# Rearranging the hand-over from an attention loop to a recurrence, and shortening the recurrence's warm-up

## Chip, cores and metric

One core of a Trainium2 chip runs the kernel. The metric is the device time of one execution in microseconds (us); the kernel before takes 3046.68 us, the median of 3 runs (3046.57 to 3047.66).

## The reference

The input x is 4 images of 128 channels by 64 x 64 positions (N = 4096 positions), float32. Cut to what matters, with the normalisations written as names:

```python
# layer 0: attention over positions, with gates, on group-normalised x
x = x + conv_bn(attention(q, k, v) * gate, Wp, sp, bp)
# layer 1: on tokens t = x with the channels last
t = t + softmax(q q^T) ln(t),  q = ln(t) @ W
# recurrence over the 4096 positions, for 4 images
Wx = batchnorm(ln(t) @ Wf.T) * gamma + beta      # statistics over all images and positions
y[i] = sigmoid(Wx[i] + V @ y[i-1]),  y[-1] = 0   # V is orthogonal (from a QR)
t = t + y                                        # the output, channels first again
```

The batch normalisation needs the mean and variance of all of Wx, so the recurrence can't start before the last attention block of the last image has gone through its layer norm and its product with Wf.

## The kernel before, in words

**Body.** For each image b the kernel does layer 0 (`layer0`, score products L238, weighted sums L476) and layer 1 (`layer1`, L726, L605, L618), 8 blocks of 512 positions each. Small jobs (normalising the next image, finishing a block) are kept in the lists `ahead` and `pending` and one is taken after each score block. Which of the emitted instructions an engine issues first is decided by a scheduler that goes by emission order and a time model, except inside a `manual_schedule` region, where every engine issues the region's instructions in the order in which they are emitted; where instructions from outside the region fall among them stays the scheduler's. `keep_in_program_order` pins one instruction behind what its engine has been given so far. Before, only the prologue (up to L797) is such a region.

**End chain.** When all parts of a block n of layer 1 are summed (`part`, L627), `finish(n)` emits four jobs: `tokens` (transposes L660, denominators L663 to L665, residual L667, layer norm L299, L300, POOL L145 and L146, L303), `turn` (transposes L680, copy by ScalarE L681, and `result`, which transposes on VectorE L275 and sends the block with 4 DMAs on SP's queue, L279) and `inputs` (product L689, statistics L690, copy L693 into `wxs`). Block 0 of the last image comes last; its jobs take their banks from the pool `ps_s`, those of the other blocks take the only bank of `ps_m`. So the jobs of blocks 2, 1 follow one another through that bank. Block 1's `turn` and `inputs` are still to run when block 0's `tokens` begins.

**Between chain and recurrence.** A first Sigmoid on ScalarE fetches the table (L827), three VectorE instructions compare all denominators with bounds (L829 to L831). Then the pools are closed and a new pool gives six PSUM banks; six products (L850) mark them as written so that later products can add to what VectorE puts there. VectorE joins the statistics (L854), POOL takes the inverse root (L145, L146), and VectorE makes `gain` and `bias` (L856 to L859).

**Recurrence.** The 4096 positions are cut into chunks of L = 32 positions that advance side by side: 4 images x 128 chunks. Each chunk first repeats the last W = 12 positions of the chunk before it as a warm-up, then does its own 32: 44 steps. A step is done in two halves of 2 images (256 columns): TensorE multiplies by V and adds into a bank that VectorE has preloaded with gain x input (`preload`, L873, two steps ahead, one instruction for each half), ScalarE applies the Sigmoid (L890). Step 0 has no product: `sigmoid(gain * wx + bias)` (L883), which is a start from y = 0. Three banks per half are used in turn. From warm-up's end plus 4 steps, VectorE adds finished results to the residual `t2s` (L900), one instruction of 512 columns for each step and four after the last one; `t2s` is loaded by 4 DMAs of 2 MB (L839) and leaves by 4 DMAs (L905), the first of which starts after the first of these last four sums. At the end (L909 to L913) the state that the warm-up reached is compared with the true one; where it differs by more than 2^-18, a `general` path recomputes everything.

**Start.** x arrives in 4 pieces of 1024 columns. While VectorE takes statistics of them, TensorE multiplies parts of x by the identity (`warm`, L781): four products ahead of the group mean's product L346, one behind it, two behind the variance's product L356. They read columns 0 to 511 of x. `normalise` (L362) overwrites these columns, then the first real product L369 reads them.

Of the kernel before, what the change touches and what calls it, by code (L numbers as in the profile page):

```python
# [10 lines left out]
F32 = mybir.dt.float32  # L11
I32 = mybir.dt.int32
AF = mybir.ActivationFunctionType
ALU = mybir.AluOpType
# [18 lines left out]
PAIRS = NT // 2  # L33
LAG = 2
SHIFT = 48.0
L, W = 32, 12
G = N // L
GB = QB // L

# [133 lines left out]
def fast(  # L173
# [10 lines left out]
    bias = keep.tile([P, 1], F32, name="bias")  # L184
    first_y = keep.tile([P, 1], F32, name="first_y")

    with ExitStack() as st:
        big = st.enter_context(tc.tile_pool(name="big", bufs=1))
        ep = st.enter_context(tc.tile_pool(name="ep", bufs=4))
        accp = st.enter_context(tc.tile_pool(name="accp", bufs=1))  # L190
        work = st.enter_context(tc.tile_pool(name="work", bufs=1))
        stat = st.enter_context(tc.tile_pool(name="stat", bufs=4))
        ps_s = st.enter_context(tc.tile_pool(name="ps_s", bufs=2, space=PSUM))
        ps_o = st.enter_context(tc.tile_pool(name="ps_o", bufs=3, space=PSUM))
        ps_m = st.enter_context(tc.tile_pool(name="ps_m", bufs=1, space=PSUM))

# [94 lines left out]
        def layernorm(src, dst):  # L293

            mv = stat.tile([P, NQ, 2], F32, tag="mv", name="mv")
            rstd = stat.tile([P, NQ], F32, tag="rstd", name="rstd")
            for j in range(NQ):
                s6 = stat.tile([P, 6], F32, tag="s6", name="s6")
                nc.vector.bn_stats(s6, src[j])  # L299
                nc.vector.bn_aggr(mv[:, j, :], s6)  # L300
            inv_sqrt(rstd, mv[:, :, 1], EPS_LN)
            for j in range(NQ):
                nc.vector.tensor_scalar(  # L303
                    dst[j], src[j], mv[:, j, 0:1], rstd[:, j : j + 1],
                    ALU.subtract, ALU.mult,
                )
# [244 lines left out]
        def layer1(b, h, qt):  # L551
# [84 lines left out]
            def finish(n):  # L636
                cs = bass.ts(n, QB)
                rinv = stat.tile([P, NQ], F32, tag="rinv", name="rinv")
                t = work.tile([P, 4, NQ, 32], F32, tag="t", name="t1", bufs=2)
                if b == B - 1 and n == 0:  # L640

                    one, two = (ep.tile([P, 2, QB], F32, tag="e", name="last") for _ in range(2))
                    h2, t1 = (one[:, r, :].rearrange("q (j c) -> q j c", j=NQ) for r in range(2))
                    th = two[:, 0, :]

                    def bank():
                        return ps_s.tile([P, 2, QB], F32, tag="s", name="ml")[:, 0, :]
                else:
                    h2 = work.tile([P, NQ, C], F32, tag="h2", name="h2")
                    th = work.tile([P, QB], F32, tag="th", name="th")  # L650
                    t1 = work.tile([P, NQ, C], F32, tag="og", name="t1b")

                    def bank():
                        return ps_m.tile([P, QB], F32, tag="m", name="m1")
                nc.sync.dma_start(t, t_d[b, n])

                def tokens():
                    m = bank().rearrange("q (j c) -> q j c", j=NQ)
                    for j in range(NQ):
                        nc.tensor.transpose(m[:, j, :], oacc[:, n, bass.ts(j, P)], ident)  # L660
                    at = (B + b) * NT + n * NQ
                    den = den_all[:, at : at + NQ]
                    nc.vector.tensor_reduce(den, m, AX.X, ALU.add)  # L663
                    nc.vector.tensor_scalar(den, den, 1.0 / C, None, ALU.mult)
                    nc.vector.reciprocal(rinv, den)  # L665
                    for j in range(NQ):
                        nc.vector.scalar_tensor_tensor(  # L667
                            t1[:, j, :].rearrange("q (p i) -> q p i", p=4),
                            m[:, j, :].rearrange("q (p i) -> q p i", p=4), rinv[:, j : j + 1],
                            t[:, :, j, :], ALU.mult, ALU.add,  # L670
                        )
                    layernorm(quarters(t1), quarters(h2))

                def result():
                    turn_out(t1.rearrange("q j (p i) -> q j p i", p=4), t2_d[b, :, cs])

                def turn():
                    m = bank()
                    for j in range(NQ):
                        nc.tensor.transpose(m[:, bass.ts(j, P)], h2[:, j, :], ident)  # L680
                    nc.scalar.copy(  # L681
                        th.rearrange("c (p j k) -> c j p k", j=NQ, p=4),
                        m.rearrange("c (j p k) -> c j p k", j=NQ, p=4),
                    )
                    result()

                def inputs():
                    m = bank()
                    nc.tensor.matmul(m, lhsT=wt["f"], rhs=th, start=True, stop=True)  # L689
                    nc.vector.bn_stats(bn_st[:, b * NB + n, :], m)  # L690
                    m = m.rearrange("p (g i s) -> p i g s", i=L // 2, s=2)
                    if b == B - 1:
                        nc.vector.tensor_copy(wxs[:, :, b, bass.ts(n, GB), :], m)  # L693
                    else:
                        wx = work.tile([P, L // 2, GB, 2], F32, tag="wx", name="wx")
                        nc.vector.tensor_copy(wx, m)
                        nc.sync.dma_start(wxs_d[b, :, :, bass.ts(n, GB), :], wx)

                if b == B - 1 and n == 0:
                    pending.appendleft(tokens)  # L700
                    pending.extend([turn, inputs])
                elif b == B - 1 and n < 4:
                    pending.extend([tokens, turn, inputs])
                else:
                    pending.extend([tokens, nothing, nothing, nothing, turn, inputs])
# [57 lines left out]
                        turned.append((clock + 4, n, a, t))  # L763
            while fifo:
                direct()
            pending.extend([reversed_products] * len(turned))

        def own_bank(_):
            return ps_m.tile([P, 512], F32, tag="m", name="mp")
# [8 lines left out]
        def warm(cols):  # L778

            m = ps_o.tile([P, QB], F32, tag="o", name="warm")  # L780
            nc.tensor.matmul(  # L781
                m[:, :cols], lhsT=ident, rhs=parts0[0][:, :cols], start=True, stop=True
            )

        for _ in range(4):
            warm(QB)
        for work_ in norm[:-2]:
            work_()
# [34 lines left out]
                ahead.popleft()()  # L823
        flush()


        tc.keep_in_program_order(nc.scalar.activation(first_y, shift, AF.Sigmoid))  # L827
        ok = big.tile([P, 2, 2 * B * NT], F32, tag="oacc", name="ok")
        nc.vector.tensor_scalar(ok[:, 0, :], den_all, DEN_LO, None, ALU.is_ge)  # L829
        nc.vector.tensor_scalar(ok[:, 1, :], den_all, DEN_HI, None, ALU.is_le)  # L830
        nc.vector.tensor_reduce(par_ok[:, 1:2], ok.rearrange("p a b -> p (a b)"), AX.X, ALU.min)  # L831


    with ExitStack() as st:
        scan = st.enter_context(tc.tile_pool(name="scan", bufs=1))
        ps_r = st.enter_context(tc.tile_pool(name="ps_r", bufs=1, space=PSUM))
        t2 = scan.tile([P, B, N], F32, name="t2s")
        for b in range(B):
            nc.sync.dma_start(t2[:, b, :], t2_d[b])  # L839
        y = scan.tile([P, L // 2, B, G, 2], F32, name="y")  # L840
        state = scan.tile([P, B, G + 1], F32, name="state")
        nc.gpsimd.memset(state[:, :, 0:1], 0.0)

        HB = B // 2
        banks = [[ps_r.tile([P, 512], F32, tag=f"r{s}{i}", name="ps_r") for i in range(3)] for s in range(2)]
        for s in range(2):
            for i in range(3):
                nc.tensor.matmul(  # L850
                    banks[s][i][:, : HB * G], lhsT=ident, rhs=wxs[:, 0, :HB, :, 0],
                    start=True, stop=True, skip_group_check=True,
                )
        nc.vector.bn_aggr(mv, bn_st.rearrange("p a b -> p (a b)"))  # L854
        inv_sqrt(gain, mv[:, 1:2], EPS_BN)
        nc.vector.tensor_mul(gain, gain, col(GAMMA))  # L856

        nc.vector.tensor_mul(bias, mv[:, 0:1], gain)
        nc.vector.tensor_sub(bias, col(BETA), bias)  # L859

        halves = [slice(s * HB, (s + 1) * HB) for s in range(2)]
        steps = list(range(L - W, L)) + list(range(L))

# [3 lines left out]
        def at(tile_, i, bs):  # L867
            return tile_[:, i // 2, bs, :, i % 2]

        def preload(k):  # L870
            if k < len(steps):
                for s, bs in enumerate(halves):
                    nc.vector.tensor_scalar(bank(k, s), at(wxs, steps[k], bs), gain, None, ALU.mult)  # L873

# [3 lines left out]
        for k, i in enumerate(steps):  # L878
            for s, bs in enumerate(halves):

                dst = state[:, bs, 1:] if k == W - 1 else at(y, i, bs)
                if k == 0:
                    nc.scalar.activation(dst, at(wxs, i, bs), AF.Sigmoid, bias=bias, scale=gain)  # L883
                    continue
                before = state[:, bs, :G] if k == W else at(y, i - 1, bs)
                nc.tensor.matmul(
# [7 lines left out]
            if k >= W:  # L894
                todo.extend((i - 3, b) for b in range(B) if i % 4 == 3)
                for j in range(len(todo) if i == L - 1 else min(1, len(todo))):
# [7 lines left out]
                    if i0 == L - 4:  # L904
                        nc.sync.dma_start(out[b], t2[:, b, :])  # L905


        gap = scan.tile([P, B, G - 1], F32, name="gap")
        nc.vector.tensor_sub(gap, state[:, :, 1:G], at(y, L - 1, slice(0, B))[:, :, : G - 1])  # L909
# [406 lines left out]
```

## Time and profile before

| | |
|---|---|
| median of 3 runs | 3046.68 us |
| profiled execution, its own time | 3047.56 us |
| its span, first to last instruction | 3045.7 us |
| TensorE busy | 2989.5 us, 98% of the span |
| VectorE, ScalarE, POOL busy | 1677.2, 1032.2, 221.0 us |
| last sum of layer 1's block 0 (L627) | 2941.69 us from the span's start |
| first Sigmoid of the recurrence (L883) | 2959.84 us |
| first step with a product: its Sigmoid (L890) | 2963.00 us |
| Sigmoid of the last step | 3018.27 us |
| first output DMA issued | 3019.60 us |
| end of the span | 3045.7 us |

A row of the timeline or of the chain of waits gives the start in us from the span's start, the duration, the engine, and what was written from what. PEld is TensorE's weight load. Each float32 product appears as two MATMUL records. PEclk is TensorE's granted clock as a share of full speed.

### The profile page before, as it was taken

The numbers are of one execution on the slowest core, as the hardware profiler recorded it, in microseconds if no ns is written. First come the engines' busy times: TensorE is split into PE (matmuls) and PEld (weight loads), VectorE is DVE, ScalarE is ACT, GpSimd is POOL, SyncE is SP. The second block draws the span as 40 slices with busy tenths as digits, with TensorE's granted clock in tenths as the row PEclk, the third lists the DMA queues.
The fourth block names the chain that finished last, engine by engine and source line by source line (L and its number), as shares of the span: only waits on it lengthen the run. The fifth ranks groups of instructions, "written<-read, shape, count | busy, mean of one in ns | idle before, by whom it ended". The sixth has DMA issues, their size and how long they took to land.

```text
span 3045.7 us, 31528 instructions
## 1 busy us (share of the span) xinstructions
PE 2989.5 (98%) x10720; PEld 1371.1 (45%) x10720; DVE 1677.2 (55%) x3114; ACT 1032.2 (34%) x1151; POOL 221.0 (7%) x215
## 2 busy tenths in 40 slices
PE   9999999999999999999999999999999999999985
PEld 4444444444444444444444444444444444444442
DVE  6666654434666664444466665443456666333356
ACT  3444432222344432222244443222234443222224
POOL 0011100000011110000011101000001111000000
PEclk9999999999999999999999999999999999999998
DMA  1112143434122123333311114343422113544333
GB/s 42 41 53 56 52 117 87 97 90 99 41 56 56 48 85 96 94 96 87 87 46 56 42 47 118 85 98 87 101 58 59 39 49 90 143 100 102 96 119 151
DMA packets 246986, 241.09 MB, mean 79 GB/s; under 512 B 90016, under 2 KB 162208, under 8 KB 245792
## 3 DMA queue, kind: packets, MB, share of 16 engines
q1 hardware_dynamic: 246816, 238.98, 29.6%
q8 instruction: 88, 1.44, 0.2%
q14 instruction: 82, 0.67, 0.1%
HBM read 65.80 MB, written 56.62 MB: 40 GB/s over the span
## 4 chain that ended last, share of the span: by engine, by line
PE 92%; DVE 3%; SPq 2%; ACT 1%; DMA 0%; issue 0%; POOL 0%; DVEq 0%; POOLq 0%; ACTq 0%
PE o L476 28%; PE o L605 15%; PE ps L238 14%; PE ps L726 14%; PE ot L618 12%; SPq L760 2%; PE m L267 1%; PE m L689 1%; PE mp L438 1%; PE ps L578 1%; PE mq L570 1%; PE mp L369 1%; PE mp L423 1%; DVE t2s L900 1%; DVE ps_r L873 1%; PE m L680 1%
## 5 line engine op out<-in xcount | busy, mean ns | idle before, releaser
L476 PE MATMUL o<-e,nxt 64*128 64x512 f32 x4096 | 973.1, 589 | 0.0
L240 ACT ACTIVATE e<-ps 128x1024 f32<-128x1024 f32 x512 | 520.9, 1023 | 687.1 <-PE ps L238 648.1
L247 DVE TENSOR_TENSOR acc<-acc,e 128x1024 f32<-128x1024 f32 x448 | 547.6, 1222 | 228.5 <-ACT e L240 212.4
L476 PEld LDWEIGHTS o<-e,nxt 64*128 64x128 f32 x4096 | 403.4, 187 | 482.9 <-issue 474.1
L238 PE MATMUL ps<-nxt 64*128 64x512 f32 x2048 | 541.6, 595 | 1.9 <-ACT e L592 0.8
L605 PE MATMUL o<-e,h 128*128 128x512 f32 x1160 | 537.0, 592 | 0.0
L730 ACT ACTIVATE e<-ps,shift 128x1024 f32<-128x1024 f32 x258 | 287.2, 1113 | 646.3 <-PE ps L726 357.9
L726 PE MATMUL ps<-qt 128*128 128x512 f32 x1032 | 482.9, 594 | 2.7 <-ACT qt L571 2.7
L618 PE MATMUL ot<-tt,h 128*128 128x512 f32 x888 | 400.9, 593 | 0.0
L733 DVE STREAM_TRANSPOSE dd<-e 128x512 f32<-128x512 f32 x444 | 281.7, 682 | 137.9 <-ACT e L730 83.7
L605 PEld LDWEIGHTS o<-e,h 128*128 128x128 f32 x1160 | 218.8, 190 | 268.2 <-issue 268.0
L238 PEld LDWEIGHTS ps<-nxt 64*128 64x128 f32 x2048 | 197.9, 187 | 231.0 <-issue 148.8
L726 PEld LDWEIGHTS ps<-qt 128*128 128x128 f32 x1032 | 189.9, 190 | 219.3 <-issue 190.8
L618 PEld LDWEIGHTS ot<-tt,h 128*128 128x128 f32 x888 | 167.8, 190 | 210.2 <-issue 205.3
L627 DVE TENSOR_TENSOR oacc<-oacc,ot 128x512 f32<-128x512 f32 x87 | 59.7, 687 | 288.4 <-PE ot L618 288.4
L145 POOL TENSOR_SCALAR rstd<-mv 128x4 f32<-128x4 f32 x64 | 14.5, 226 | 2374.9 <-DVE mv L300 2374.9
L532 DVE SCALAR_TENSOR_TENSOR t<-yt,rinv,t 128x128 f32<-128x128 f32 x128 | 36.5, 347 | 80.2 <-DMA yt<-turn_d 80.2
L493 POOL TENSOR_SCALAR xb<-xb,bpc 128x512 f32<-128x512 f32 x32 | 61.6, 1924 | 243.9 <-DMA xb<-in_x_dram 234.3
L543 POOL TENSOR_SCALAR h<-h 128x512 f32<-128x512 f32 x32 | 72.3, 2261 | 63.7 <-DVE d L275 61.7
L588 ACT ACTIVATE e<-ps,shift 128x512 f32<-128x512 f32 x32 | 22.0, 687 | 144.1 <-PE ps L584 133.8
L146 POOL TENSOR_TENSOR rstd<-rstd,mhalf 128x4 f32<-128x4 f32 x64 | 66.4, 1037 | 5.3
L629 DVE COPY oacc<-ot 128x512 f32<-128x512 f32 x24 | 16.6, 691 | 85.6 <-PE ot L618 85.5
(156 smaller groups left out, 1611.2 us busy)
## 6 DMA issues: line engine op xcount, KB each, us to landing
tt<-dd SPq DMA_DIRECT2D x1776, 64.0 KB, 2.0
turn_d<-d SPq DMA_DIRECT2D x384, 64.0 KB, 1.8
nxt<-in_x_dram SPq DMA_DIRECT2D x16, 512.0 KB, 5.6
xb<-in_x_dram SPq DMA_DIRECT2D x32, 256.0 KB, 3.3
t<-turn_d SPq DMA_DIRECT2D x32, 256.0 KB, 2.7
yt<-turn_d SPq DMA_DIRECT2D x32, 256.0 KB, 2.7
t_d<-t SPq DMA_DIRECT2D x32, 256.0 KB, 2.0
qt<-turn_d SPq DMA_DIRECT2D x32, 256.0 KB, 2.9
```

The costliest lines, as they stand in the source:

```text
L146: nc.gpsimd.tensor_tensor(dst, dst, mhalf[:, :n], ALU.pow)
L238: nc.tensor.matmul(ps[:, h, :], lhsT=lhsT, rhs=rhs, start=True, stop=True)
L240: nc.scalar.activation(e, ps, AF.Exp, scale=scale)
L247: nc.vector.tensor_tensor(acc, acc, e, ALU.add)
L476: nc.tensor.matmul(o[r], lhsT=v[rs, p + h * PAIRS, :], rhs=e[rs, h, :], start=(p == 0 and h == 0), stop=(p == PAIRS - 1 and h == 1),)
L493: biased = nc.gpsimd.tensor_scalar(xb, xb, bpc, None, ALU.add)
L543: nc.gpsimd.tensor_scalar(hn, hn, 1.0, None, ALU.add)
L605: nc.tensor.matmul(o, lhsT=h[:, NQ * a + 2 * i + half, :], rhs=e[:, half, :], start=(a == order(n)[0] and i == 0 and half == 0), stop=(a = ...
L618: nc.tensor.matmul(ot, lhsT=h[:, NQ * n + j, :], rhs=t[:, :, j, :, :].rearrange("q p k j -> q k p j"), start=(j == 0), stop=(j == NQ - 1),)
L726: nc.tensor.matmul(ps[:, half, :], lhsT=qt[:, bass.ts(at, P)], rhs=qt[:, bass.ts(n, QB)], start=True, stop=True,)
L730: nc.scalar.activation(e, ps, AF.Exp, bias=shift)
L733: nc.vector.transpose(d.rearrange("q f b k j -> q k b f j")[:, 2 * i + half], e[:, half, :].rearrange("q (b f j) -> q b f j", b=NQ, f=NQ),)
```

## The change

The kernel after differs in these places.

- **Warm-up:** W is 10 instead of 12, so 42 steps. Step 0 starts from y = 1/2: its bias is `first_bias`, which is `bias` plus V times a column of 1/2 (one product with one column, `of_half`).
- **Region:** after the last weighted sum of the last image a `manual_schedule` region begins; it is closed ahead of the recurrence. In it, in written order: block 0's `tokens`, `turn`, `inputs`, the product `of_half`, the table's Sigmoid, the joined statistics, the inverse root, the copy of block 0's inputs (now after the statistics: `last_inputs`), and five small VectorE operations that make `first_bias`, `gain` and `bias`.
- **Banks:** the loop's PSUM pools stay open. Block 0's jobs use `ps_o`. The recurrence's six banks are the two double banks of `ps_s`, one of `ps_o` and the one of `ps_m`; they are taken and marked in block 0's `tokens` right behind its transposes (`take_banks`), each mark being a product that reads the constant `bc`.
- **Products for the clock:** `busy(4)`, four products of 512 columns into one of these banks, after the marks and again after `of_half`. At the start `warm` reads columns 1536 to 2047 (the second piece), and two of its products stand ahead of the mean instead of four.
- **Joint scaled inputs:** where a step's two banks are the two of one `ps_s` tile (two steps of three) one VectorE instruction of 512 columns preloads both halves.
- **Layer norm:** `bn_aggr` of a tile is emitted one `bn_stats` later.
- **Block 1:** one empty job stands between its `tokens` and `turn`.
- **Denominator check:** emitted behind the recurrence.

```diff
-L, W = 32, 12
+L, W = 32, 10
...
+    half = keep.tile([P, 1], F32, name="half")
+    nc.gpsimd.memset(half, 0.5)
+    first_bias = keep.tile([P, 1], F32, name="first_bias")
...
-        ps_s = st.enter_context(tc.tile_pool(name="ps_s", bufs=2, space=PSUM))
-        ps_o = st.enter_context(tc.tile_pool(name="ps_o", bufs=3, space=PSUM))
-        ps_m = st.enter_context(tc.tile_pool(name="ps_m", bufs=1, space=PSUM))
+        ps_s = keep_ctx.enter_context(tc.tile_pool(name="ps_s", bufs=2, space=PSUM))
+        ps_o = keep_ctx.enter_context(tc.tile_pool(name="ps_o", bufs=3, space=PSUM))
+        ps_m = keep_ctx.enter_context(tc.tile_pool(name="ps_m", bufs=1, space=PSUM))
...
+            sums: deque = deque()
             for j in range(NQ):
                 s6 = stat.tile([P, 6], F32, tag="s6", name="s6")
                 nc.vector.bn_stats(s6, src[j])
-                nc.vector.bn_aggr(mv[:, j, :], s6)
+                sums.append((mv[:, j, :], s6))
+                if j > 0:
+                    nc.vector.bn_aggr(*sums.popleft())
+            nc.vector.bn_aggr(*sums.popleft())
...
                     def bank():
-                        return ps_s.tile([P, 2, QB], F32, tag="s", name="ml")[:, 0, :]
+                        return ps_o.tile([P, QB], F32, tag="o", name="ml")
...
                         nc.tensor.transpose(m[:, j, :], oacc[:, n, bass.ts(j, P)], ident)
+                    if b == B - 1 and n == 0:
+                        take_banks()
...
-                    if b == B - 1:
+                    if b == B - 1 and n == 0:
+                        last_inputs.append(m)
+                    elif b == B - 1:
                         nc.vector.tensor_copy(wxs[:, :, b, bass.ts(n, GB), :], m)
...
+                elif b == B - 1 and n == 1:
+                    pending.extend([tokens, nothing, turn, inputs])
...
             while fifo:
                 direct()
+            if b == B - 1:
+                ordered.enter_context(tc.manual_schedule())
...
+        def mark(m, cols):
+            nc.tensor.matmul(
+                m[:, :cols], lhsT=ident, rhs=bc.rearrange("p a c -> p (a c)")[:, :cols],
+                start=True, stop=True, skip_group_check=True,
+            )
+
+        def take_banks():
+            for i in (1, 2):
+                pair = ps_s.tile([P, 2, QB], F32, tag="s", name="ps_r")
+                pairs[i] = pair
+                for r in range(2):
+                    banks[r][i] = pair[:, r, :]
+            banks[0][0] = ps_o.tile([P, QB], F32, tag="o", name="ps_r")
+            banks[1][0] = ps_m.tile([P, QB], F32, tag="m", name="ps_r")
+            for r in range(2):
+                for i in range(3):
+                    mark(banks[r][i], HB * G)
+            busy(4)
+
+        def busy(times):
+            for _ in range(times):
+                mark(banks[0][0], QB)
...
-                m[:, :cols], lhsT=ident, rhs=parts0[0][:, :cols], start=True, stop=True
+                m[:, :cols], lhsT=ident, rhs=parts0[0][:, 1536 : 1536 + cols], start=True, stop=True
...
-        for _ in range(4):
+        for _ in range(2):
             warm(QB)
...
+        of_half = banks[0][1][:, QB - 1 :]
+        nc.tensor.matmul(
+            of_half, lhsT=wt["vt"], rhs=half, start=True, stop=True, skip_group_check=True
+        )
+        busy(4)
+
+        nc.scalar.activation(first_y, shift, AF.Sigmoid)
+        nc.vector.bn_aggr(mv, bn_st.rearrange("p a b -> p (a b)"))
+        inv_sqrt(gain, mv[:, 1:2], EPS_BN)
+        nc.vector.tensor_copy(wxs[:, :, B - 1, :GB, :], last_inputs[0])
+        nc.vector.tensor_add(first_bias, of_half, col(BETA))
+        nc.vector.tensor_mul(gain, gain, col(GAMMA))
+
+        nc.vector.tensor_mul(bias, mv[:, 0:1], gain)
+        nc.vector.tensor_sub(first_bias, first_bias, bias)
+        nc.vector.tensor_sub(bias, col(BETA), bias)
+        ordered.close()
...
         def preload(k):
-            if k < len(steps):
+            if k >= len(steps):
+                return
+            if k > 1 and pairs[k % 3] is not None:
+                nc.vector.tensor_scalar(
+                    pairs[k % 3][:, :, : HB * G].rearrange("p r (b g) -> p r b g", g=G),
+                    at(wxs, steps[k], slice(0, B)).rearrange("p (r b) g -> p r b g", r=2),
+                    gain, None, ALU.mult,
+                )
+            else:
                 for s, bs in enumerate(halves):
                     nc.vector.tensor_scalar(bank(k, s), at(wxs, steps[k], bs), gain, None, ALU.mult)
...
-                    nc.scalar.activation(dst, at(wxs, i, bs), AF.Sigmoid, bias=bias, scale=gain)
+                    nc.scalar.activation(dst, at(wxs, i, bs), AF.Sigmoid, bias=first_bias, scale=gain)
```

The removed lines that the diff above leaves out are the old marks (L846 to L853), the old making of `gain` and `bias` (L854 to L859) and the denominator check (L827 to L831), whose three VectorE lines come again, unchanged, behind the recurrence.

More of the change, by code (lines that the diff above doesn't have):

```diff
@@ L765, in layer1 @@
                 direct()
+            if b == B - 1:
+                ordered.enter_context(tc.manual_schedule())
             pending.extend([reversed_products] * len(turned))
+        HB = B // 2
+        banks = [[None] * 3 for _ in range(2)]
+        pairs = [None] * 3
+        last_inputs = []
+        ordered = ExitStack()
+        def mark(m, cols):
[18 more added lines that the diff above has]
+                mark(banks[0][0], QB)
         def own_bank(_):
@@ L824, in fast @@
         flush()
[L827 to L831, printed above, removed]
+        of_half = banks[0][1][:, QB - 1 :]
[13 more added lines that the diff above has]
+        ordered.close()
     with ExitStack() as st:
         scan = st.enter_context(tc.tile_pool(name="scan", bufs=1))
-        ps_r = st.enter_context(tc.tile_pool(name="ps_r", bufs=1, space=PSUM))
         t2 = scan.tile([P, B, N], F32, name="t2s")
@@ L842, in fast @@
         nc.gpsimd.memset(state[:, :, 0:1], 0.0)
[L846 to L859, printed above, removed]
         halves = [slice(s * HB, (s + 1) * HB) for s in range(2)]
@@ L905, in fast @@
                         nc.sync.dma_start(out[b], t2[:, b, :])
+        ok = scan.tile([P, 2, 2 * B * NT], F32, name="ok")
+        nc.vector.tensor_scalar(ok[:, 0, :], den_all, DEN_LO, None, ALU.is_ge)
+        nc.vector.tensor_scalar(ok[:, 1, :], den_all, DEN_HI, None, ALU.is_le)
+        nc.vector.tensor_reduce(par_ok[:, 1:2], ok.rearrange("p a b -> p (a b)"), AX.X, ALU.min)
         gap = scan.tile([P, B, G - 1], F32, name="gap")
```

## The prediction

> **What bounds the kernel now.** I read the page first, then the chain of waits over the last 150 us, then VectorE's and TensorE's timelines there and at the start, then the granted clock us by us. The page says that the body is out of play:
>
> ```profile
> PE 2989.5 (98%) x10720; PEld 1371.1 (45%) x10720; DVE 1677.2 (55%) x3114; ACT 1032.2 (34%) x1151; POOL 221.0 (7%) x215
> ```
>
> TensorE is busy nearly always until the last block; the change removes no product there. What it can move lies at both ends. The chain of waits from the last block to the recurrence (start, duration, what):
>
> ```profile
> 2949.77 1.04 POOL rstd L146
> ...
> 2951.24 1.26 PE ml L680 x4
> 2952.52 0.59 ACT last L681
> 2953.16 2.09 PE ml L689 x2
> 2955.27 0.70 DVE bn_st L690
> 2955.97 0.60 DVE wxs L693
> 2956.57 0.14 issue
> 2956.70 5.46 PE ps_r L850 x12
> 2962.16 0.81 PE ps_r L886 x2
> ```
>
> The reader is to see that the six bank marks (L850, 12 records, 5.46 us) end the wait for the first product of the recurrence, and that L680 and L689 take long: L689 needs 2.09 us here and 0.94 us for block 2. The windows tell why (columns: stretch, busy time of PE, PEld, DVE, ACT, POOL, then PEclk):
>
> ```profile
> 2948.00:2949.00 1.00, 0.00 (x0) 0.00 (x0) 1.00 (x7) 0.00 (x0) 0.00 (x0) 1.00 0.00 0
> 2949.00:2950.00 1.00, 0.00 (x0) 0.00 (x0) 0.97 (x4) 0.00 (x0) 0.46 (x2) 0.56 0.00 0
> ...
> 2962.00:2963.00 1.00, 1.00 (x4) 0.82 (x3) 0.49 (x1) 0.00 (x1) 0.00 (x0) 0.61 1.05 434
> 2963.00:2964.00 1.00, 0.88 (x4) 0.31 (x3) 0.48 (x2) 0.94 (x2) 0.00 (x0) 1.00 0.99 426
> ```
>
> The clock halves at about 2949.1, 3 us after the last product, and is full again at 2962.8. In the recurrence the chain is first a loop of TensorE and ScalarE, later VectorE alone:
>
> ```profile
> 2970.77 0.49 ACT y L890
> 2971.27 0.04 issue
> 2971.31 0.73 PE ps_r L886 x2
> 2972.04 0.02 issue
> 2972.07 0.49 ACT y L890
> ...
> 3008.15 0.59 DVE t2s L900
> 3008.74 0.78 DVE ps_r L873 x2
> 3009.53 0.59 DVE t2s L900
> ...
> 3017.78 3.60 DVE t2s L900 x6
> ```
>
> One step takes 1.30 us in the loop (2970.77 to 2972.07) and 1.375 us where VectorE's sum and two preloads (0.59 + 0.78) fill it. At the start, VectorE's timeline has
>
> ```profile
> 14.50 1.00 DVE L362 TENSOR_SCALAR nxt<-nxt,gdev 128x512 f32<-128x512 f32 x2 [1.24 <-PE warm L781]
> ```
>
> so normalising waits for the last warm product, which reads the columns it overwrites.
>
> **What the Trainium skill says.** TensorE: Matmul & The Clock Gate, Part 1 (The HAM clock gate): TensorE runs at half rate by default, goes to full after a busy window of about 3.4 us and back after an idle one; the windows run free of the kernel. The trace agrees on the halves (0.86 us for a 512-column pass at the start, 0.43 us later), and the drop and the rise, 13.7 us apart, fit four windows. But the window before the drop held 0.43 us of product, so it needn't be empty; and one with products from 2956.7 on, about 2.7 us of 3.4, brought no rise. VectorE: DVE Perf Modes, Why PSUM operands drop a tier: float32 with a PSUM operand runs at one element a cycle. L873's 482 ns for 256 columns agree with 0.27 us plus a fixed part. No page settles the order that the scheduler will choose.
>
> **The change, part by part.** All sums are against the profiled execution (3047.56 us; its span 3045.7 us and 1.9 us around it); the savings then come off the median, 3046.68 us.
>
> 1. *Two warm-up steps.* 2 x 1.295 = 2.6 us. Sure.
>
> 2. *Joint inputs.* A preload of 256 columns advances VectorE by 0.39 us, 0.27 of it columns. 512 columns give 0.53 + 0.12 = 0.66 us (bounds 0.52 at double rate, 0.75 with no overlap). Three steps then cost 2 x 0.66 + 0.78 + 3 x 0.59 = 3.88, or 1.29 us a step, level with the loop. Before, from the first product's Sigmoid (2963.00) to the last (3018.27) there are 42 steps of 1.316 on average, 0.9 us above the loop: VectorE falls behind from the first sum on, but being two steps ahead it hides about 1.4 us. That 0.9 us goes, plus 0.1 before the first output DMA. With 0.75 about 0.4 us stays. The joint instruction must wait for both halves of the step before, yet has over 1 us in hand. Next limit: the TensorE-ScalarE loop. Parts 1 and 2: 3.6 us (3.1 to 3.8).
>
> 3. *From block 0's product to the first looped step.* Before, L689's end (2955.23) to that step's Sigmoid (2963.00) is 7.77 us. After: statistics 0.65 with the hand-over, join (L854) to gain 2.02 (2956.48 to 2958.50, POOL's part in it unchanged), three operations of 0.2 and the way to ScalarE 0.72, Sigmoid of half a step 0.57 with hand-over, product 0.77 at full clock: 4.8 us. The copy (0.60) and the sum for `first_bias` (0.2) lie in POOL's 1.0 us; the table load (1.28) lies under the statistics. Queued behind L689 on TensorE are `of_half` and four products, 0.3 + 8 x 0.43 = 3.7 us; the looped product is ready after 4.0. They hide, by 0.3 us, at full clock only. A preload may slip between the small operations, as one did before at 2959.13 (0.4 us). Gain 2.7 us (2.3 to 3.0).
>
> 4. *Block 0's chain up to that product.* On VectorE, L275 (0.59), L829 (0.1) and some hand-overs leave the chain; POOL's wait now hides nothing needed. But TensorE becomes late: the sixth bank is block 1's, free when its copy L693 is done (2947.46 before). Layer norm in its new order closes the gap into which L275 had slipped ahead of block 1's last L300 (2940.65), worth 0.4 us until another sum stands in the way: 2947.0. Behind that wait stand three marks (6 x 0.215 = 1.3 us) and eight passes (3.4), and behind them L680, at 2951.8 against 2951.24. VectorE would have been ready at 2949.6, so the products for the clock cost 2 us here. In return the clock is full: L680 to L689's end takes 0.6 + 0.6 + 1.1 + 0.1 = 2.4 instead of 4.0 us. Sum 2954.2 against 2955.23, gain 1.0 us (bounds -0.5 and 2.0 by how the scheduler places L690 and L693).
>
> 5. *Start.* L346 waited for the fourth early product until 11.20; with two it can go at 11.0. L362 no longer waits (14.50), it can go at 13.55 behind POOL. At full clock L369 starts at 14.2 instead of 15.10: gain 0.9. But now TensorE's early activity is 4 x 0.86 = 3.4 us, from the second piece's arrival (about 6.3) to 9.75, then 1.2 us idle. Before, it ran without a gap from 5.18. To fill a window it would have to fall on one almost exactly. If it doesn't, the later products run at half clock, the six passes behind the mean and the variance end at 15.5 to 16.7, and L369 starts 0.4 to 1.6 us later than before: take -1.0. I hold the loss likelier (6 to 4).
>
> 6. *The rest.* The three check instructions (0.26 + 0.26 + 0.69) are behind the output DMAs, which run from 3019.6 to about 3041; SP's queue has nothing behind them. Block 0's four DMAs now follow the normalising, landing around 2955, ahead of the first write to `y` (2957.6), and `t2s`'s loads, 21 us, end around 2976.3 against a last first use at about 2979. Nothing, though without the 2.7 us in hand VectorE would stall. The warm-up stays long enough: the Sigmoid's slope is at most 1/4 and V keeps lengths, so ten steps shrink the distance by at least 4^10.
>
> Sum: 3.6 + 2.7 + 1.0 - 1.0 = 6.3 us: **3040.4 us**.
>
> **Rivals.**
> - *Good start:* the early products fill a window. For: they last just 3.4 us. Against: random phase. 1.9 us better, 3038.5.
> - *The bank comes late:* L690 and L693 land behind block 0's statistics (about 1 us), or the wait on TensorE (1.4 us or more between L689 and the mark) lets the clock fall for a window, costing half of 3.4 us. For: windows one-third busy did drop (the one ending at 3020.8). Against: two-thirds busy ones didn't. 2.7 us worse, 3043.1.
> - *Slower than before:* the inserted products run at half clock through both stages. Marks and passes take 2.7 + 6.9 us, so L680 starts at 2956.6, L689 ends at 2960.7 as slowly as before, and `of_half` with 6.9 us of passes puts the looped Sigmoid at about 2969, 6 us later than 2963.00. With 3.6 gained and 1.0 lost at the start: 3050.1. It turns to a loss when more than two-thirds of these passes are slow. Against: they are themselves the activity that raises the clock.
> - *Joint inputs do nothing*, should the bank pair make one half wait for the other: 0.9 us less, inside the range.
>
> **How the numbers follow.** A measurement of this kernel tells about 0.2% (6.1 us) from no change, so the line lies at 3040.6. Forecast 42%, good start 27%, late bank 21%, slow clock 5%, an unforeseen order of the scheduler 5% (either side, up to 8 us). Faster by over 0.2%: six in ten of the first, nearly all of the second, none of the third, some of the last: 0.54. Slower by over 0.2% only where the last two meet: 0.03. The rest, 0.43. Range: 3037.3 (good start with part 4 at its best) to 3044.3 (late bank with a poor start and a slip in part 3).
>
> **What would show it.** L680 of block 0 near 2951.8 and L689 at 1.1 us, full PEclk from 2942 on; 4.8 us from L689's end to the first looped Sigmoid; 40 steps of 1.30 to the last; a joint preload of 0.75 us; L362 at 13.6 or 14.5 and L369's start. It is wrong if PEclk shows a half in the end chain, if TensorE still stands in its queue when the first `y` is ready, or if the steps stay at 1.37.

## The result and the profile after

The kernel after takes 3054.38 us (median of 14 runs, 3052.93 to 3059.47) against 3046.74 us for the kernel before (14 runs, 3045.65 to 3047.66): ratio 1.0027, 95% interval 1.0019 to 1.0036. It is 0.27% slower, where 3040.4 us and a gain were forecast. Its profiled execution took 3056.14 us, with a span of 3054.4 us, 8.7 us more than before.

The body is as it was. The engines' line of the page:

```profile
PE 2988.7 (98%) x10726; PEld 1371.7 (45%) x10726; DVE 1672.9 (55%) x3085; ACT 1030.7 (34%) x1147; POOL 224.3 (7%) x216
```

The chain of waits from the last block to the recurrence (start, duration, what; the diff moves L680, L689 and L886 to L690, L699 and L937):

```profile
2948.84 5.00 PE ps_r L797 x14
2953.83 0.45 PE ml L690 x4
...
2954.95 1.14 PE ml L699 x2
...
2959.28 0.30 DVE ok L960
...
2959.84 0.40 DVE ps_r L924
...
2961.09 0.44 issue
2961.52 0.70 PE ps_r L937 x2
```

The clock is full here: L699's product takes 1.14 us, where L689's took 2.09. Marks and fillers (L797) hold TensorE until block 0's transposes. Between `gain` and `bias` stands an instruction that was to come behind the recurrence, the denominators' test (L960), and a preload (L924) stands ahead of `first_bias`.

The same view inside the recurrence, two steps of the kernel after:

```profile
2963.55 0.95 ACT y L941 x2
2964.49 0.04 issue
2964.53 0.73 PE ps_r L937 x2
2965.27 0.02 issue
2965.29 0.49 ACT y L941
```

Before, product (0.73) and one Sigmoid (0.49) took turns, 1.30 us for a step. Now two Sigmoids in a row (0.95) lie on the path in two steps of three: the second half's of one step and, behind it on ScalarE, the first half's of the next. The second half's product of that next step (2964.53) begins only when the first half's Sigmoid of the same step has ended (2964.49), which its numbers don't need; the timeline names the wait:

```profile
2964.53 2.47 PE L937 MATMUL ps_r<-y,w 128*128 128x256 f32 x8 [0.58 <-ACT y L941]
```

Such a step takes 1.75 us (2963.55 to 2965.29). These are the steps whose two banks share one tile; the third, in single-bank tiles, still takes 1.30. The first products of the body, at the other end, in the timeline:

```profile
14.97 1.00 DVE L370 TENSOR_SCALAR nxt<-nxt,gdev 128x512 f32<-128x512 f32 x2 [0.52 <-POOL gdev L146]
...
16.37 1.02 PE L377 MATMUL mp<-nxt,w 128*128 128x512 f32 x2
```

Normalising no longer waits for a warm product but for POOL; still, the first real product starts 1.27 us later than before (15.10), because most of the warm products ahead of it ran at half clock (L832's last four took 2.92 us, 1.96 for the same ones before).

Where the span's 8.7 us come from, each by a difference of times in the two traces:

| stretch | before | after | difference |
|---|---|---|---|
| start of the span to block 0's last sum (L627, now L635) | 2941.69 | 2942.84 | +1.15 |
| that sum to the end of block 0's product (L689, now L699) | 13.54 | 13.23 | -0.31 |
| that end to the first looped Sigmoid | 7.77 | 6.18 | -1.59 |
| first looped Sigmoid to the last step's | 55.27 (42 steps of 1.316) | 64.29 (40 of 1.607) | +9.02 |
| last step's Sigmoid to the end of the span | 27.5 | 27.9 | +0.4 |

### The profile page after: what moved, and what is told of

It reads as the page before. It is cut to its first block, busy times and chain, and to the rows that moved or that the text cites. A ratio compares the mean times of both kernels' runs of the same rounds, so it can differ in the third digit from the quotient of the medians.

```text
span 3054.4 us, 31476 instructions
## 1 busy us (share of the span) xinstructions
PE 2988.7 (98%) x10726; PEld 1371.7 (45%) x10726; DVE 1672.9 (55%) x3085; ACT 1030.7 (34%) x1147; POOL 224.3 (7%) x216
## 4 chain that ended last, share of the span: by engine, by line
PE 90%; SPq 3%; DVE 2%; ACT 2%; DMA 1%; issue 1%; POOL 0%; DVEq 0%; ACTq 0%
PE o L484 28%; PE o L613 15%; PE ps L242 14%; PE ps L740 13%; PE ot L626 12%; SPq L774 3%; ACT y L941 1%; PE ps_r L937 1%; PE m L271 1%; PE m L699 1%; PE mp L446 1%; PE ps L586 1%; PE mp L377 1%; PE mq L578 1%; PE mp L431 1%
## 5 line engine op out<-in xcount | busy, mean ns | idle before, releaser
L635 DVE TENSOR_TENSOR oacc<-oacc,ot 128x512 f32<-128x512 f32 x87 | 59.8, 687 | 287.9 <-PE ot L626 287.9
L937 PE MATMUL ps_r<-y,w 128*128 128x256 f32 x160 | 47.4, 415 | 19.1 <-ACT y L941 15.7
```

Source lines behind the costliest of these rows:

```text
L937: nc.tensor.matmul(bank(k, s), lhsT=wt["vt"], rhs=before, start=False, stop=True, skip_group_check=True,)
```

## Experiments

All times are medians of several runs; "first" and "last" are the starts of the first looped Sigmoid and of the last step's in the profiled execution. Unless said otherwise each kernel is the kernel after with the edit shown. The runs of before beside them had medians of 3046.3 to 3047.2 us.

**Is it the joint instruction?** Two preloads for each step; the pair tiles stay.

```diff
-            if k > 1 and pairs[k % 3] is not None:
-                ...
-            else:
-                for s, bs in enumerate(halves):
-                    nc.vector.tensor_scalar(bank(k, s), ...)
+            for s, bs in enumerate(halves):
+                nc.vector.tensor_scalar(bank(k, s), ...)
```

> The kernel after, with every preload in two instructions of 256 columns; the banks stay the two of one ps_s tile. Theory (shared tile): in two of three steps the second half's product waits for the first half's Sigmoid because both banks lie in one tile, so the 40 looped steps still take about 64 us (1.61 each) and the time stays at 3054 (3052.5 to 3056). Rival (joint instruction): the 512-column preload ties the halves, so the steps fall to 1.30 to 1.32 us, 53 us together, and the time to about 3043.

3054.43 us (ratio to before 1.0027, 1.0016 to 1.0039), 40 steps of 1.61. Nothing changes, so the joint instruction is not what costs. The shared tile is what is left.

**Is it two halves in one tile?** In addition each pair tile now holds two banks of the same half.

```diff
-                    banks[r][i] = pair[:, r, :]          # tile i holds both halves
+                    banks[r][i] = pair[:, i - 1, :]      # tile r holds two steps of half r
```

> The kernel after, but each ps_s tile gives both of its banks to one half of the images, with preloads of 256 columns. Shared tile: the halves are free of each other, steps of 1.30 to 1.38 us, 52.5 to 55 us for 40 of them, time 3042.5 to 3045.5; a preload can now be held by the Sigmoid of one step later, which may cost up to 1 us. Rival (taking the banks from the loop's pools is itself the cost): unchanged at 3054.

3050.27 us (1.0009, 1.0000 to 1.0018), 40 steps of 1.488: better by 4.2 us, but short of what was expected. Its chain of waits:

```profile
2963.79 1.34 DVE ps_r L916 x3
2965.13 0.14 issue
2965.27 0.70 PE ps_r L929 x2
```

The halves are free of each other, but now a preload for one step waits for the Sigmoid of another step in the same tile, and every third product waits for that preload. The tie has moved; it goes where the tile is shared. The expectation had named this wait, but at up to 1 us; against single-bank tiles (next experiment) the 40 steps take 6.2 us more, most of it in the late steps, where the preload that was held also stands behind an addition and every third step takes 2.03 us.

**Tiles of one bank each.** The pool `ps_s` is closed in `take_banks` and its banks come back as four tiles of one bank.

```diff
-            for i in (1, 2):
-                pair = ps_s.tile([P, 2, QB], F32, tag="s", name="ps_r")
-                ...
+            ps_s_ctx.close()
+            ps_r = keep_ctx.enter_context(tc.tile_pool(name="ps_r", bufs=1, space=PSUM))
+            for r in range(2):
+                for i in (1, 2):
+                    banks[r][i] = ps_r.tile([P, QB], F32, tag=f"r{r}{i}", name="ps_r")
```

> The kernel after, but the pool ps_s is closed in take_banks and four tiles of one bank each take its place, with preloads of 256 columns. Shared tile: waits as in the kernel before, steps of 1.30 in the first part and 1.375 once VectorE is full, 52.7 us for 40 steps, time 3042 to 3044. Rival (loop's banks): 3054. If the pool's change costs a wait in the end chain, it shows ahead of the first mark.

3044.54 us (0.9995, 0.9988 to 1.0002), 9.8 us below the kernel after and 0.5 above the range expected; 40 steps of 1.332 (first 2959.96, last 3013.23), and in the chain of waits one Sigmoid for each product again:

```profile
2963.86 0.49 ACT y L935
2964.35 0.04 issue
2964.39 0.73 PE ps_r L931 x2
```

The four banks are those that the closed pool gives back, and the instructions of a step are those of the kernel with two preloads; what differs is into how many tiles the banks are divided. The time was in the tie by tile.

**The same part alone, on the kernel before.** Pair tiles and joint preloads, nothing else of the change.

```diff
-        banks = [[ps_r.tile([P, 512], F32, tag=f"r{s}{i}", name="ps_r") for i in range(3)] for s in range(2)]
+        pairs = [None] + [ps_r.tile([P, 2, 512], F32, tag=f"p{i}", name="ps_r") for i in (1, 2)]
+        banks = [[ps_r.tile([P, 512], F32, ...)] + [pairs[i][:, s, :] for i in (1, 2)] for s in range(2)]
...         # and the joint preload of the kernel after
```

> The kernel before with one part alone: the banks of two of three steps come as pairs in one tile each, preloaded by one joint instruction; W stays 12. Shared tile: 42 looped steps at 1.61 instead of 1.316, plus 12 us, 3058 to 3060. Rival (the loss needs the loop's banks, the region or the short warm-up): no slower than before, 3046 to 3047, or 1 us faster.

3061.27 us (1.0049, 1.0032 to 1.0066), 42 steps of 1.607. The part alone costs 14.9 us, more than the 12 expected: in the profiles 12.2 lie in the steps, as expected, and 1.4 behind the last Sigmoid. So it outweighs all that the rest of the change brings. The other experiments ask what that rest is worth; they start from the kernel with single banks.

**The warm-up.** `W = 12` again.

> Single banks with twelve warm-up steps instead of ten, started from 1/2 as with ten. Both theories of the forecast agree here: two more steps at 1.33 us (40 steps took 53.27 us), so 2.65 us more, 3047.2 us; less than 2 us more would say that steps at the start are cheaper than those of the middle.

3046.46 us. First to last Sigmoid is 55.26 us for 42 steps against 53.27 for 40: two steps are worth 1.99 us, not 2.6. The steps at the start do take 1.30; but with ten warm-up steps the last 17 take 1.375, with twelve only the last 11, and 6 x 0.075 is 0.45 us, most of the 0.6 that is missing.

**What the slow steps wait for.** Every second addition of y to `t2s` inside the recurrence goes to GpSimd.

```diff
-                    nc.vector.tensor_tensor(
+                    adder = nc.gpsimd if b % 2 and i < L - 2 else nc.vector
+                    adder.tensor_tensor(
```

> Single banks, every second addition of y to t2 inside the recurrence on GpSimd instead of VectorE. In the single-bank kernel the last 17 of 40 steps take 1.375 us instead of 1.30, and in each of them the product waits 0.23 us for a preload that stands behind an addition of 0.68 us. Theory: VectorE is the bound of these steps (0.86 for two preloads and 0.68 for an addition, less what overlaps), so all 40 steps take 1.30 us, 1.3 us less: 3043.2 us. Rival: the additions only take slack, and the slower step is TensorE's and ScalarE's own: 3044.5 us, or more if GpSimd's additions hold VectorE up.

3041.55 us (0.9981, 0.9974 to 0.9988); first 2961.70, last 3013.60, so 40 steps of 1.298. VectorE was the bound of the late steps, and 1.4 us of recurrence go, as expected. The median fell by 3.0 us, though. In the profile another 1.5 us are gone behind the last Sigmoid (27.3 us against 28.8 with single banks): the four output DMAs are issued within 0.1 us of the same place behind it, but the last one lands 1.5 us sooner. Over the profiles of this study that stretch takes 27.3 to 28.9 us; what decides it stays open. (Its profiled execution started late, at 16.00, which the next but one explains.)

**Order on VectorE.** The denominators' test and the first preloads are pinned.

```diff
-        nc.vector.tensor_scalar(ok[:, 0, :], den_all, DEN_LO, None, ALU.is_ge)
+        tc.keep_in_program_order(nc.vector.tensor_scalar(ok[:, 0, :], den_all, DEN_LO, None, ALU.is_ge))
...         # the second comparison, and the preloads of steps 1 and 2, likewise
```

> Single banks, with the test on the denominators kept behind the recurrence and the first preloads kept in written order. In the single-bank kernel this test stands between the gain (ends at 2956.96 us) and the bias (2957.77), 0.6 us of it issue before the test itself. If that issue is the wait for the buffer the test writes to, the step from the gain to the first Sigmoid shrinks by 0.8 us, 3043.7 us. Rival: the same waits then stand before the first addition of y to t2 inside the recurrence, where a preload stands behind it, and a step of the loop grows by up to 0.6 us: 3044.5 us.

3043.46 us (0.9990, 0.9983 to 0.9997). From the start of `gain` to step 0's Sigmoid 0.97 us instead of 1.74, so the expected 0.8 us; the step of the loop didn't grow. One preload still falls ahead of `first_bias` and keeps 0.4 us.

**Early products for the clock.** Twenty small products of the identity matrix with itself, then six on x, in place of two on x.

```diff
-        for _ in range(2):
-            warm(QB)
+        for _ in range(5):
+            m = ps_o.tile([P, NQ, P], F32, tag="o", name="warm")
+            for j in range(NQ):
+                nc.tensor.matmul(m[:, j, :], lhsT=ident, rhs=ident, start=True, stop=True)
+        for i in (1536, 1536, 1536, 512, 512, 512):
+            m = ps_o.tile([P, QB], F32, tag="o", name="warm")
+            nc.tensor.matmul(m, lhsT=ident, rhs=parts0[0][:, i : i + QB], start=True, stop=True)
```

> Single banks, and twenty products of 128 columns on the identity matrix from about 1.4 us on, then three products on each of two pieces of x, so that TensorE has work from about 1.5 to 9.5 us without a gap. Clock theory (the start is lost or won by when the full clock is granted, and two warm-up products too few leave it open): the products of this stretch come down from 0.94 us to about 0.5 us before 8 us, the first real product starts at 14.2 us in the profile, and the median is 3043.5 us, within 0.5. Rival (the group mean on VectorE sets the start in any case): first real product still between 15 and 16 us where the clock is late, median 3044.5 us as with single banks.

3045.86 us, and the runs lie within 0.9 us, where those with single banks spread over 4.3. The full clock came at 6.1 us, ahead of the 8 us expected (the passes that start up to 5.84 us still take 0.421 us; the 5.6 us that a later expectation names is a misreading). But each float32 product is two passes; I had counted one, so the last of them held the group mean's product until 13.37 and the first real product started at 16.55. The spread is the start's; the price was my miscount.

**Fillers.** Two instead of four behind the marks (`busy(2)`), then none at all, neither there nor behind `of_half`.

> Single banks, two filler products instead of four behind the marks of the banks. In the single-bank kernel block 0's normalised block is ready at 2950.42 us, but its transposes start at 2951.59, when the fillers end. Theory: the fillers hold TensorE; two end by 2949.9, the transposes start at about 2950.5, 1.1 us earlier, and the last product's end with them, if the clock stays full: 3043.4 us. Rival: the idle half microsecond takes the full clock away, the transposes and L700's product double (0.60 and 1.12 us), and 0.6 us are lost: 3045.1 us.

3042.75 us (0.9988, 0.9981 to 0.9995). Block 0's product starts at 2951.34 instead of 2952.87, with both starts of the body within 0.12 us, and at full clock: 1.4 us less. In this kernel the scheduler also put the test on the denominators behind `bias`, which gives 0.8 us more.

> Single banks, without any filler: neither the four behind the marks nor the four behind the product by 1/2 (the six marks stay). Theory of the forecast: TensorE is then idle for about 2 us before block 0's transposes and for 4 us before the first step, the full clock goes, the transposes and L700's product double (1.7 us more, against 1.4 saved by the free engine) and the first steps of the recurrence have products at half clock: 3046.5 us or more. Rival: the clock outlasts these gaps, and only the 1.4 us saved are left: 3043.1 us.

3043.01 us (0.9988, 0.9981 to 0.9995). Neither expectation holds whole. Block 0's transposes (1.09 us) and its product (1.12) keep the full clock without fillers, though TensorE is idle for 1.38 us ahead of the marks and for 1.38 again behind them. But the 4.33 us of idle TensorE ahead of the recurrence lose it. Stretches of 2 us, columns as in the forecast, PEclk third from the end:

```profile
2956.00:2958.00 2.00, 0.96 (x2) 0.83 (x3) 2.00 (x8) 1.12 (x2) 0.00 (x0) 0.52 0.83 295
2958.00:2960.00 2.00, 2.00 (x6) 1.14 (x5) 1.97 (x6) 0.99 (x2) 0.00 (x0) 0.50 0.97 418
```

The first three looped steps take 1.81, 1.79 and 1.51 us, and the last Sigmoid comes 1.8 us after that with two fillers (3012.78 and 3010.93, bodies 0.09 us apart). So in these profiles `busy` behind `of_half` earns 1.8 us. The medians of the two kernels are only 0.3 us apart and their intervals are the same, so this size rests on one profile of each; the three slow steps are plain. `busy` behind the marks earns nothing: block 0's product starts at 2951.47 without fillers and at 2951.34 with two, and four cost 1.4 us.

**The mends together.** Single banks; twelve small products and five on x at the start; pinned order; `busy(2)`.

> Single banks with three mends together: TensorE busy without a gap from 1.4 us to about 10.6 us at the start (twelve small products on the identity matrix, five on x; in the kernel with early products the full clock came at 5.6 us, but its last ones held the group mean back by 2.4 us), the test on the denominators and the first preloads in written order, and two fillers instead of four. Clock theory: the full clock before 7 us in every run, first real product at 14.2 us, and the runs within 1.5 us of each other; with 0.8 us from the order and 1.4 from the fillers below the good runs of single banks (3043.7): 3041.5 us. Rival: the spread of the runs (5 us with single banks) is not the start's, and the median is 3042.3 with the same spread.

3039.76 us (0.9976, 0.9968 to 0.9984), the runs from 3039.41 to 3041.39. TensorE's timeline of the start:

```profile
1.42 5.31 PE L840 MATMUL warm<-ident 128*128 128x128 f32 x24 [1.42 <-POOL ident masks.py:199]
6.57 4.46 PE L843 MATMUL warm<-nxt,ident 128*128 128x512 f32 x10
```

There is no gap until the group mean's product at 10.87, ten passes take 4.46 us (at half clock four took 3.75), and the first real product starts at 14.13. The runs spread over 2.0 us, a little more than expected, and less than half of what single banks had. It is the fastest version of the study, 14.6 us below the kernel after. It is also 1.7 us better than expected: in the profile the first looped Sigmoid comes 2.2 us earlier than with single banks (2957.76), which is what the order and the fillers were to give, and about 1.0 more is gone behind the last Sigmoid, unexplained as above. Last, the same with every second addition on GpSimd:

> The kernel with the three mends, and every second addition of y to t2 inside the recurrence on GpSimd. Theory (the gains are at different places and add up): 3039.8 us of the three mends less the 1.4 us that the recurrence lost to VectorE, so 3038.4 us, all 40 steps at 1.30 us, the runs within 2 us of each other. Rival: earlier steps meet the load of t2 or the last additions, and half of it or more comes back after the last Sigmoid: 3039.1 to 3039.8 us.

3040.80 us (0.9980, 0.9971 to 0.9989): the rival's side, and more. The first 28 steps take 1.30, but four late ones 1.5 to 2.0, because there a preload stands behind an addition of 1.79 us and a product waits 0.82 us for it; the last Sigmoid is at 3011.21, no earlier than without the edit (3011.05). Behind it 0.6 us more pass than without the edit (28.35 against 27.77). What made the same edit pay in one kernel and not in the other, beyond where the additions fell, stays open.

## Why the prediction was wrong

**The step that failed** is in part 2: "The joint instruction must wait for both halves of the step before, yet has over 1 us in hand. Next limit: the TensorE-ScalarE loop." It asked what the joint *instruction* waits for. It didn't ask what waits when two banks are one *tile*: the second half's product, which writes into the tile, has to wait for the first half's Sigmoid, which reads from it. The halves then take turns instead of overlapping: product 0.73, two Sigmoids 0.95, hand-overs 0.06, 1.75 us in place of 1.30, in 27 of 40 steps. 27 x 0.45 is 12.2 us; measured against 40 steps of 1.30 it was 12.3. The fourth rival named just this wait ("should the bank pair make one half wait for the other"), but its price, 0.9 us, was the joint preloads' gain foregone; the loop's own loss was left out. Priced from the chain that the forecast itself shows (0.73, 0.49 and the second Sigmoid), it would have been the rival on the slower side. The Trainium skill's page PSUM — Partial Sum Buffer (section PSUM bank collisions raise a hardware error) tells of a dependency between engines that touch the same bank and partitions. Here the halves lie in two banks. The trace has the wait nevertheless (0.58 us before each such product), and the same banks in tiles of their own don't have it.

The kernel did turn out slower, but not by the way of the rival *Slower than before*: that one had the inserted products at half clock, and here the end chain ran at full clock (L699 1.14 us).

The other steps, each in us:

- *Part 1, two steps 2.6, "Sure":* 2.0 with single banks (twelve steps again). VectorE's slow stretch starts six steps earlier. Too sure, mechanism right.
- *Part 2, the joint preload:* 0.75 us, the upper bound. The 0.9 that VectorE costs in the late steps is real, and with ten warm-up steps it is 1.4 (additions shared with GpSimd). Joint inputs as written here couldn't have it, since they need both banks in one tile; their worth without the tie wasn't tried.
- *Part 3, L689's end to the looped Sigmoid 4.8:* 6.18. Of the difference 0.8 is the denominators' test ahead of `bias` (what pinning it gave with single tiles), 0.4 the preload ahead of `first_bias`, which the forecast named as a danger; 0.2 goes with single tiles (5.96 there). With single tiles, two fillers and the better order the stretch is 5.2, and the preload is all that is left of the miss.
- *Part 4, gain 1.0:* 0.31. The bank of block 1 came free 0.6 later than forecast in the body's own time (2948.79 less 1.15 is 2947.6, against 2947.0): the 0.4 that the layer norm's new order was to give didn't come, as the transposition (L279, before L275) slipped in ahead of block 1's last aggregate again (2941.73), and two marks stand among block 1's transposes (2944.78), 0.2 more. That the fillers cost time there was right, 2 us by the forecast, 1.4 by the two-filler kernel; that they are needed there was not.
- *Part 5, the start -1.0 or +0.9, six to four for the loss:* both kinds occur. A late start began at 16.0 to 17.0 in the profiles, five times of nine with these two warm products, a good one at 14.1 to 14.2, four times; one of the late ones, 1.9 us behind 15.10, lies beyond the 1.6 forecast. Which of the two a profile shows is chance, so the close figure in the sum below is luck. That the clock's windows run free of the kernel, as the Trainium skill's page TensorE: Matmul & The Clock Gate says in Part 1 (The HAM clock gate), agrees: the same start lands on either side, and in the three kernels with TensorE busy from 1.4 on no profile had the half clock at the first real product.
- *Part 6, nothing:* two of its readings were off without changing the sum. The last load of `t2s` lands 23 us after the first one's issue, not 21 (2979.44), still ahead of the first addition (2981.93); and the output DMAs of the kernel before land up to 3043.92, not about 3041.

Summed up on the profiled executions: the forecast's span is 3045.7 - 6.3, 3039.4, and the measured one is 15.0 longer. Of this 12.5 is the recurrence (3.5 that were to be gained there, 9.0 lost), 1.1 part 3, 0.7 part 4, 0.15 the start, and the rest lies behind the last Sigmoid. With that one wait priced at 12.3 the forecast would have read 3052.7.

## What to carry to other kernels

When two buffers that were apart are put into one tile, ask of every reader and writer of either, not only of the instruction that wanted them together, what it now waits for; two pipelines that overlapped may come to take turns, and that price falls due in every such step. Before a filler product is put in, find the idle stretch that it covers: here one of 4.3 us was worth filling, by the profiles, and one of 1.4 us wasn't. And an instruction that is only *written* later is not later: what matters is where the scheduler puts it in its engine's queue.

## What was not expected of the hardware

- With TensorE busy without a gap from 1.41 us, the passes of 128 columns came down from 0.421 to 0.275 us at 6.0 to 6.4 us in three profiles, 4.6 to 5.0 us after the start. Four passes of 512 columns over 3.75 us, followed by about 1 us of idle, brought the full clock by 10.6 us in four profiles and not in five.
- The full clock outlasted two idle stretches of 1.38 us close together, and fell in one of 4.33 us (no fillers).
- Where additions are shared (2980 to 3012 us, single banks), one of 128x512 takes 1.54 us in the median on GpSimd, and on VectorE 0.68 to 1.58, 1.08 in the median. Where GpSimd has none of them, VectorE takes 0.68.
